# Shorter rests on GpSimd between indirect transfers in a routed mixture of experts

## The chip, the cores and the metric

The kernel runs on one core of a Trainium2 chip. The metric is the device time of one execution in microseconds (us). A profile of one further execution comes with the runs. The engines are called PE (TensorE), DVE (VectorE), ACT (ScalarE), POOL (GpSimd) and SP (SyncE, which here only issues DMAs); PEld is the weight load of PE.

## The reference, cut to what matters

Eight blocks are applied one after another to 2048 tokens of 128 numbers (8 sequences of 256), each as `x = layernorm(x + block(x))`: attention and feed-forward blocks L0 to L3. The change lies in the sixth, a mixture of 160 experts of which each token takes 8:

```python
def _L2_ffn_ref(hidden_states, router_w, expert_bias, w_gate, w_down, w_gate_shared, w_down_shared):
    ...
    probs = jax.nn.sigmoid(x @ router_w.T + expert_bias[None, :])
    top_w, top_idx = jax.lax.top_k(probs, 8)
    top_w = top_w / (jnp.sum(top_w, axis=-1, keepdims=True) + 1e-09) * 2.5
    combine = zeros(T, 160) with top_w at top_idx
    h1 = jax.nn.silu(jnp.einsum('th,eih->eti', x, w_gate))
    routed = jnp.einsum('eti,ehi->th', h1 * combine.T[:, :, None], w_down)
    return routed + silu(x @ w_gate_shared.T) @ w_down_shared.T
```

The block after it (L3 attention) is six layers of linear attention and a feed-forward of 512; the last (L3 ffn) is attention with weights of several widths.

## The kernel before, in words

The tokens are four groups of 512 (`GT`), held as tiles of 128 partitions x 4 x 128. Two groups make a half: `first` is groups 0 and 1, `second` groups 2 and 3. The halves go through the blocks staggered, so that one half's work can run beside the other's.

In the routed experts the work of a half has four steps:

- `plan` counts the tokens of each expert and gives every (token, choice) pair a row in a table in DRAM, `placed[h]`. Rows are grouped in tiles of 64 of one expert, eight tiles to a block. `place` then scatters the tokens: for each group 4 x 8 indirect DMAs on GpSimd (L622), each of 128 rows of 512 bytes, so 64 per half.
- `routed_experts` runs 36 blocks: 20 with one tile for each of the 160 experts, 16 with the tiles that overflow, whose experts are known only at run time. A block loads its rows (`xb`, L702) and weights (L713, L714, or eight loads at L719), turns the rows (L725), multiplies (L729, L740) and writes the results to a second table, `made[h]` (L743, issued by ACT). A block that is not used skips its transfers. Weights and rows have two buffers each. The load of the first block waits for all the scatters of its half.
- `gather` fetches for each token its eight rows from `made[h]` (L751), again 64 indirect DMAs per half, into `got` (two buffers of eight), and DVE adds them up, weighted (L757). It waits for the last write of `made[h]`.
- The normalized sum goes to the six layers of L3 attention (matmuls at L1106 to L1171; the feed-forward of a layer is L1165 and L1171).

`pause` (L541 is its `memset`) stands behind every indirect DMA: fills of a scratch tile `idle` (128 x 176) on GpSimd, tied in order to the transfer before and the transfer behind, so that GpSimd rests between two transfers. Nothing reads `idle`.

The order of the program around it, from the end of the kernel's body:

```python
            stage(run, l2_route, first)
            plan(first)
            l1_experts(second)
        routed_experts(first)
        ...
        stage(run, l2_route, second)
        plan(second)
        gathers(first)
        es.close()
        layers = l3_attn(ctx)
        run = layers(first)
        routed_experts(second)
        ...
        gathers(second)
```

`plan(h)` holds the scatters of the half. `l3_attn(ctx)` issues the loads of the L3 weights on SP's queue (L63, L69). Each engine runs its instructions in an order fixed when the program is built by a scheduler with a cost model; `behind` adds an order without a wait.

Of the kernel before, what the change touches and what calls it, by code (L numbers as in the profile page):

```python
# [42 lines left out]
def tile_post_ln_blocks(ctx: ExitStack, tc: tile.TileContext, I, out: bass.AP):  # L43
    nc = tc.nc
    V, S, G, PE = nc.vector, nc.scalar, nc.gpsimd, nc.tensor
# [98 lines left out]
    def tokens(g, src):  # L144
        t = xs[g].tile([P, 4, D], F32, tag="x", name="x")
        normalize(g, t, src)
        return t
# [384 lines left out]
    def behind(ins, other, why):  # L532

        tc.add_manual_dep(
            ins, other.name, mybir.DependencyInfo(mybir.DependencyClass.NoSync, mybir.DependencyReason.DATA), reason=why
        )

    def pause(after):

        for _ in range(3):  # L540
            after, last = G.memset(idle, 0.0).ins, after  # L541
            behind(after, last, "a rest between transfers")
        rest[0] = after

# [20 lines left out]
    def plan(half):  # L565

        n = EXPERTS

        def t(tag, dt=F32):
            return pp.tile([P, n], dt, tag=tag, name=tag)  # L570

        c0, c1 = (count[g] for g in half)
        whole, size, end, jump = t("whole", U32), t("size"), t("end"), t("jump")
        V.tensor_tensor(size, c0, c1, ALU.add)
        V.tensor_scalar(size, size, TILE - 1.0, TILE - 1.0, ALU.add, ALU.max)
        V.tensor_copy(whole, size)
        V.tensor_scalar(whole, whole, 0xFFFFFFFF - (TILE - 1), None, ALU.bitwise_and)

        V.tensor_scalar(size, whole, -float(TILE), 0.0, ALU.add, ALU.max)
        V.tensor_tensor_scan(end, ones, size, 0.0, ALU.mult, ALU.add)  # L580
        et = pp.tile([P, 1], F32, tag="et", name="et")
        own = t("own_c")
        V.scalar_tensor_tensor(own, end, tile_at, ones, ALU.is_le, ALU.mult, accum_out=et)
        pe = bank(lanes[0].ps)[:1, :P]
        PE.transpose(pe, et, ident)
        ei = pp.tile([1, P], I32, tag="ei", name="ei", bufs=2)
        V.tensor_copy(ei, pe)

        V.tensor_tensor(end, end, size, ALU.subtract)
        V.scalar_tensor_tensor(jump, end, TILE * (n - 1.0), first_at, ALU.add, ALU.subtract)  # L590
        placing[half[0] // 2] = []
        tile_of[half[0] // 2] = ei
        for g, c in zip(half, (None, c0)):
            place(lanes[g % 2], g, c, jump)

    def place(ln, g, before, jump):
        n, k, h = EXPERTS, TOP, g // 2
        at = upto[g]
        if before is not None:
            V.tensor_tensor(at, at, before.unsqueeze(1).to_broadcast([P, 4, n]), ALU.add)  # L600
        far = parts(ln, "gw", n)[0]
        V.scalar_tensor_tensor(
            far, at, float(TILE), jump.unsqueeze(1).to_broadcast([P, 4, n]), ALU.is_gt, ALU.mult
        )
        V.tensor_tensor(at, at, first_at.unsqueeze(1).to_broadcast([P, 4, n]), ALU.add)
        V.tensor_tensor(at, at, far, ALU.add)
        V.tensor_tensor(at, at, chosen[g], ALU.mult)
        p8 = ln.pick.tile([P, 4, 8], F32, tag="p8", name="p8")
        for j in range(4):
            V.max(out=p8[:, j, :], in_=at[:, j, :])  # L610

        p, q, rw = (ln.pick.tile([P, 4, k], U32, tag=f"pl{i}", name=f"pl{i}") for i in range(3))
        V.tensor_scalar(p, p8[:, :, :k], -1.0, None, ALU.add)
        V.tensor_scalar(rw, p, P - 1, 2, ALU.bitwise_and, ALU.logical_shift_left)
        V.tensor_scalar(q, p, 7, 3, ALU.logical_shift_right, ALU.bitwise_and)
        V.tensor_tensor(rw, rw, q, ALU.bitwise_or)
        V.tensor_scalar(p, p, 0xFFFFFFFF - (TILE * BLOCK - 1), None, ALU.bitwise_and)
        V.tensor_tensor(rw, rw, p, ALU.bitwise_or)
        row[g] = rw
        for j in range(4):  # L620
            for c in range(k):
                i = G.indirect_dma_start(  # L622
                    placed[h][:, :], bass.IndirectOffsetOnAxis(rw[:, j, c : c + 1], 0), x[g][:, j, :], None
                ).ins
                group = f"place{h}"
                if placing[h]:
                    tc.declare_no_dep(i, group=group, reason="no two tokens have the same row")
                tc.add_to_no_dep_group(group, i)
                placing[h].append(i)
                if rest[0] is not None:  # L630
                    behind(i, rest[0], "a rest between transfers")
                pause(i)
        placed_at[g] = at, p8

    def shares(ln, g):
# [109 lines left out]
    def gather(ln, g):  # L745

        y = sums[g]
        for j in range(4):
            got = gp.tile([P, 8, D], F32, tag="got", name="got")
            for c in range(TOP):  # L750
                i = G.indirect_dma_start(  # L751
                    got[:, c, :], None, made[g // 2][:, :], bass.IndirectOffsetOnAxis(row[g][:, j, c : c + 1], 0)
                ).ins
                behind(i, rest[0], "a rest between transfers")
                pause(i)
            for c in range(TOP):
                V.scalar_tensor_tensor(  # L757
                    y[:, j, :], got[:, c, :], share[g][:, j, c : c + 1], y[:, j, :], ALU.mult, ALU.add
                )
        x[g] = tokens(g, y)  # L760
# [22 lines left out]
    def parts(ln, tag, *sizes):  # L783

        t = ln.work.tile([P, sum(4 * n for n in sizes)], F32, tag=tag, name=tag)
        at, out = 0, []
        for n in sizes:
            out.append(t[:, at : at + 4 * n].rearrange("p (a b) -> p a b", b=n))
            at += 4 * n
        return out  # L790
# [580 lines left out]
    def gathers(half):  # L1371
        for g in half:
            gather(lanes[g % 2], g)

    with ExitStack() as moe:
# [9 lines left out]
        idle = mw.tile([P, 176], F32, tag="idle", name="idle")  # L1385
# [64 lines left out]
    last = l3_ffn(ctx)  # L1450
# [140 lines left out]
```

## Time and profile before

| | us |
|---|---|
| median of 3 runs | 2006.09 |
| lowest, highest | 2005.3, 2006.96 |
| profiled execution, device time | 2013.03 |
| its span in the trace | 2011.1 |

| engine | busy us | share of the span |
|---|---|---|
| PE | 1742.4 | 87% |
| PEld | 1166.6 | 58% |
| DVE | 1211.9 | 60% |
| ACT | 889.9 | 44% |
| POOL | 453.2 | 23% |

The profiled execution takes 1.9 us more than its span. Times in the trace are from the start of the span. Of POOL's time, 191.6 us are the 768 fills of L541 (249 ns each), 127.5 us the 128 scatters of L622 and 123.2 us the 128 gathers of L751. The profile's duration of an indirect DMA is the time that POOL is occupied by it; its data land later.

### The profile page before, as it was taken

How to read it: one execution, taken by the hardware profiler on the slowest of the kernel's cores; microseconds unless marked ns; L12 is line 12 of the kernel's file. 1: busy time of each engine (PE TensorE's matmuls, PEld its weight loads, DVE VectorE, ACT ScalarE, POOL GpSimd, SP SyncE). 2: the span in 40 equal slices, each digit the busy share in tenths (PEclk: the TensorE clock that was granted, in tenths of full speed). 3: DMA queues.
4: the chain of work that ended last, by engine and by line, in shares of the span. 5: the costliest groups of instructions: out<-in, count | busy, mean ns of one | idle time of the engine just before them, and what ended most of it. 6: DMA issues, size and time to landing. Idle time of an engine off the chain costs nothing.

```text
span 2011.1 us, 38559 instructions
## 1 busy us (share of the span) xinstructions
PE 1742.4 (87%) x13996; PEld 1166.6 (58%) x13996; DVE 1211.9 (60%) x3920; ACT 889.9 (44%) x1992; POOL 453.2 (23%) x1041
## 2 busy tenths in 40 slices
PE   9999889977999999999879672677967799999887
PEld 6888644554555446644467451556745677666554
DVE  4000356876878756799558720455576777766663
ACT  4555434724755345642424210133444466555543
POOL 1000000000000000007870688883088400000000
PEclk9999989988999999999789866778988899999997
DMA  3000078502333642336118765777011000000000
GB/s 100 4 3 4 22 227 255 168 0 59 105 100 99 164 128 76 100 106 188 46 44 262 239 192 175 236 223 219 31 33 32 19 1 1 1 1 6 6 1 11
DMA packets 161486, 185.38 MB, mean 92 GB/s; under 512 B 20336, under 2 KB 118512, under 8 KB 161296
## 3 DMA queue, kind: packets, MB, share of 16 engines
q1 hardware_dynamic: 143264, 149.86, 25.9%
q0 software_dynamic: 8192, 16.79, 2.7%
q10 hardware_dynamic: 9840, 16.26, 2.2%
q8 instruction: 111, 1.82, 0.4%
q14 instruction: 79, 0.65, 0.1%
HBM read 143.69 MB, written 56.16 MB: 99 GB/s over the span
## 4 chain that ended last, share of the span: by engine, by line
PE 60%; POOL 17%; DVE 10%; DMA 5%; issue 4%; ACT 4%; SPq 0%; ACTq 0%; POOLq 0%; DVEq 0%
PE ps_s L360 8%; POOL idle L541 7%; PE ps_o L427 7%; PE ps_m L432 7%; POOL placed L622 6%; PE ps_m L437 4%; PE ps L136 4%; PE ps L1171 4%; POOL got L751 3%; PE ps L1165 3%; PE ps_s L279 2%; DMA got<-made,pl 2%; PE ps L956 2%; PE ps L1294 2%; PE ps_o L740 1%
## 5 line engine op out<-in xcount | busy, mean ns | idle before, releaser
L622 POOL DMA_INDIRECT placed<-x,pl x128 | 127.5, 996 | 998.5 <-DMA wu<-in_F_wu_dram 903.6
L434 ACT ACTIVATE h<-ps_m 128x512 f32<-128x512 f32 x196 | 116.0, 597 | 235.7 <-PE ps_m L432 213.6
L427 PE MATMUL ps_o<-h,wd 128*128 128x512 f32 x384 | 200.9, 607 | 7.8 <-DVE h L440 7.8
L432 PE MATMUL ps_m<-xT,wg 128*128 128x512 f32 x384 | 197.9, 598 | 3.0 <-ACT h L434 3.0
L541 POOL MEMSET idle<- 128x176 f32 x768 | 191.6, 249 | 29.7
L360 PE MATMUL ps_s<-st,L_a 128*64 128x32 f32 x4096 | 193.2, 222 | 1.1
L360 PEld LDWEIGHTS ps_s<-st,L_a 128*64 128x64 f32 x4096 | 160.7, 137 | 29.9 <-ACT st L369 12.3
L440 DVE TENSOR_TENSOR h<-h,bc 128x512 f32<-128x512 f32 x192 | 131.4, 686 | 48.8 <-ACT h L434 40.3
L369 ACT ACTIVATE st<-ps_s 128x64 f32<-128x64 f32 x512 | 114.2, 223 | 102.6 <-PE ps_s L360 71.1
L751 POOL DMA_INDIRECT got<-made,pl x128 | 123.2, 963 | 104.3 <-DMA made<-ob 78.3
L437 PE MATMUL ps_m<-xT,wu 128*128 128x512 f32 x256 | 133.8, 605 | 4.2 <-ACT h L434 2.8
L740 PE MATMUL ps_o<-w,xg 64*64 64x128 f32 x1152 | 102.1, 331 | 37.6 <-DVE xg L735 37.4
L427 PEld LDWEIGHTS ps_o<-h,wd 128*128 128x128 f32 x384 | 73.2, 195 | 96.9 <-issue 66.6
L432 PEld LDWEIGHTS ps_m<-xT,wg 128*128 128x128 f32 x384 | 71.2, 191 | 84.7 <-issue 64.7
L438 DVE TENSOR_TENSOR h<-h,ps_m 128x512 f32<-128x512 f32 x132 | 89.9, 681 | 46.8 <-PE ps_m L437 43.3
L740 PEld LDWEIGHTS ps_o<-w,xg 64*64 64x64 f32 x1152 | 80.4, 165 | 57.0 <-DVE xg L735 46.8
L317 DVE SCALAR_TENSOR_TENSOR outsT<-xnT,L_skip,ps 128x64 f32<-128x64 f32 x32 | 10.4, 324 | 168.2 <-PE ps L305 168.2
L742 ACT COPY ob<-ps_o 128x512 f32<-128x512 f32 x72 | 42.1, 585 | 154.8 <-PE ps_o L740 139.5
L136 PE MATMUL ps_m<-ident,xb 128*128 128x128 f32 x288 | 57.5, 333 | 58.9 <-DMA xb<-placed 58.9
L757 DVE SCALAR_TENSOR_TENSOR yb<-got,w,yb 128x128 f32<-128x128 f32 x128 | 44.3, 346 | 103.4 <-DMA got<-made,pl 102.9
L1165 PE MATMUL ps<-nT,A_w 128*128 128x512 f32 x192 | 98.1, 632 | 9.5 <-ACT nT L1091 5.2
L1171 PE MATMUL ps<-A_w,hT 128*128 128x128 f32 x768 | 99.1, 281 | 6.5 <-DVE hT L1167 6.4
(370 smaller groups left out, 3603.5 us busy)
## 6 DMA issues: line engine op xcount, KB each, us to landing
bc<-comb SPq DMA_DIRECT2D x128, 256.0 KB
w<-in_F_w_dram SPq DMA_DIRECT2D x256, 96.0 KB
placed<-zero SPq DMA_DIRECT2D x72, 256.0 KB
xb<-placed SPq DMA_DIRECT2D x72, 256.0 KB
made<-ob ACTq DMA_DIRECT2D x72, 256.0 KB
w<-in_F_wg_dram SPq DMA_DIRECT2D x40, 256.0 KB
w<-in_F_wd_dram SPq DMA_DIRECT2D x40, 256.0 KB
bc<-comb SPq DMA_DIRECT2D x16, 512.0 KB
```

What stands on the lines that cost most here:

```text
L136: PE.transpose(ps[:, j, :], src[:, j, :], ident)
L360: in_turn(PE.matmul(now[h][sides[c], n % HB // 2, n % 2, s].rearrange("p e f b -> p (e f b)"), lhsT=a_sb[:, n % 2, 4 * h + k, :], rhs=prev ...
L427: PE.matmul(acc[g], lhsT=w, rhs=h, start=begin, stop=end, skip_group_check=True)
L432: PE.matmul(pg, lhsT=wg, rhs=xT[g], start=True, stop=True)
L437: PE.matmul(pu, lhsT=wu, rhs=xT[g], start=True, stop=True)
L440: V.tensor_tensor(h, h, bc[:, i * GT : (i + 1) * GT], ALU.mult)
L541: after, last = G.memset(idle, 0.0).ins, after
L622: i = G.indirect_dma_start(placed[h][:, :], bass.IndirectOffsetOnAxis(rw[:, j, c : c + 1], 0), x[g][:, j, :], None).ins
L740: PE.matmul(po[k, i // 2, :], lhsT=h[k, i // 2, :], rhs=wd[i], start=True, stop=True)
L751: i = G.indirect_dma_start(got[:, c, :], None, made[g // 2][:, :], bass.IndirectOffsetOnAxis(row[g][:, j, c : c + 1], 0)).ins
L1165: PE.matmul(ph, lhsT=w1[:, f * P : (f + 1) * P], rhs=nT, start=True, stop=True)
L1171: PE.matmul(po[:, j, :], lhsT=hT[:, f, j * P : (j + 1) * P], rhs=w2[:, f, :], start=(f == 0), stop=(f == 3),)
```

## The change

The rest becomes a parameter. Behind the scatters of the first half it stays three fills of 176 columns; behind those of the second half and behind the gathers of both halves it becomes two fills of 112 columns.

```diff
-    def pause(after):
-
-        for _ in range(3):
-            after, last = G.memset(idle, 0.0).ins, after
+    def pause(after, fills=3, columns=176):
+
+        for _ in range(fills):
+            after, last = G.memset(idle[:, :columns], 0.0).ins, after
             behind(after, last, "a rest between transfers")
         rest[0] = after
...
-                pause(i)
+                pause(i, *((3, 176), (2, 112))[h])
...
-                pause(i)
+                pause(i, *((2, 112), (2, 112))[g // 2])
```

## The prediction

> **What bounds the kernel now.** I read the chain of waits first, to see whether POOL is on the path at all.
>
> ```profile
> PE 60%; POOL 17%; DVE 10%; DMA 5%; issue 4%; ACT 4%; SPq 0%; ACTq 0%; POOLq 0%; DVEq 0%
> ```
>
> POOL is busy for only 23% of the span, but 17% of the chain is POOL's: 7% the fills of `idle` (L541), 6% the scatters (L622), 3% the gathers (L751). The chain in order of time is POOL nearly throughout 911 to 1045 us (first scatter, left as it is), 1117 to 1248 (second scatter), and much of 1455 to 1586 (second gather). Then the timeline of POOL, for one transfer and its rest:
>
> ```profile
> 1119.70 0.96 POOL L622 DMA_INDIRECT placed<-x,pl  x1 [0.16 <-issue]
> 1120.66 0.86 POOL L541 MEMSET idle<- 128x176 f32 x3
> 1121.69 0.96 POOL L622 DMA_INDIRECT placed<-x,pl  x1 [0.16 <-issue]
> ...
> 1483.14 0.95 POOL L751 DMA_INDIRECT got<-made,pl  x1 [0.16 <-issue]
> 1484.09 0.86 POOL L541 MEMSET idle<- 128x176 f32 x3
> ```
>
> Columns: start, duration, what, idle before it. A transfer costs 0.96 + 0.86 (three fills) + 0.16 = 1.98 us. Every eighth gap is 0.48, so the 64 of the second scatter take 1117.71 to 1247.8, 2.03 each. Nothing but POOL's own stream paces them. Next, the busy time by stage, for what happens beside it (PE, PEld, DVE, ACT, POOL, then granted clock, DMA share, GB/s):
>
> ```profile
> 1180.00:1218.00 38.00, 30.77 (x332) 23.59 (x332) 9.74 (x18) 8.71 (x18) 31.00 (x73) 0.81 0.38 121
> 1218.00:1251.00 33.00, 0.51 (x10) 0.27 (x6) 0.00 (x0) 0.58 (x1) 27.55 (x65) 0.56 0.73 226
> 1455.00:1587.00 132.00, 92.62 (x442) 65.33 (x440) 91.52 (x339) 53.66 (x127) 110.24 (x256) 0.87 0.11 33
> 1587.00:2011.00 424.00, 386.35 (x2354) 265.61 (x2354) 283.71 (x918) 226.32 (x537) 0.00 (x0) 0.94 0.01 3
> ```
>
> From 1218 to 1251 everything but POOL stands still: the first half's experts are done, the second half's tokens are not placed. After 1587 PE is 91% busy. The timeline of SP's queue says what it does in the hole:
>
> ```profile
> 1216.19 0.34 SPq L63 DMA_DIRECT2D A_wk<-in_A_wk_dram  x1
> ...
> 1235.84 0.38 SPq L714 DMA_DIRECT2D w<-in_F_wd_dram  x1
> 1248.35 4.30 SPq L702 DMA_DIRECT2D xb<-placed  x3
> ```
>
> From 1216 to 1236 it issues the L3 weights and the first two expert blocks' weights, one per 0.47 us; then it waits for the scatter until 1248.35 (the waits of SP's queue put 11.9 us down to it). The last wait that matters:
>
> ```profile
> POOL got L751 <- DMA made<-ob: 78.3, 1, 78.3
> ```
>
> The second gather starts at 1455.08, when the second half's experts have written their last block. So the order is: second scatter, experts of the second half (1250 to 1455), second gather (1455 to 1586), then 425 us in which PE is nearly full.
>
> **The price of a fill.** No row has 112 columns. The groups by shape give 98 ns for 128x1, 194 for 128x128, 249 for 128x176, 327 for 128x256. From 176 down at the slope 128-to-176 (1.15 ns a column) 112 cost 175; at the slope 176-to-256 (0.98) 186; from 128 down toward 128x1 (0.76) 182. I take 182. In a triple the fills are 0.27, 0.25, 0.24 with gaps of 0.05. Two of 112: 0.27 + 0.05 + 0.25 less 2 x 0.067 = 0.44, against 0.86. Saved: 0.42 us per transfer (0.40 to 0.44 by the other slopes), 27 us in each of the three stages (64 transfers each).
>
> That assumes the gap of 0.16 stays and the transfer stays at 0.96, and the trace has no transfer with less rest. Bounds: at worst the whole 0.42 comes back as waiting on POOL (saving 0), or the transfers stretch to 1.61, the longest in the first scatter (a loss of 0.23 each). I take no change, since all gaps within the scatter but one (1.49) are 0.16 or 0.48 whatever else runs, and the transfers average 964, 956 and 970 ns in the three stages, though the DMA share is 0.66, 0.73 and 0.11 there.
>
> By the Trainium skill, "DMA: Bandwidth & Descriptors", Anatomy of one DMA, a transfer from this queue has a fixed cost of about 2.0 us, mostly completion; transfers spaced by that would gain nothing here, because 1.98 is already it. The trace disagrees for spacing: the transfer at 1276.24 takes 3.43 us to land, and the next is issued at 1278.20, before that. Latency overlaps here.
>
> **Second scatter.** The last of 64 transfers starts at 1245.97 now; 63 x 0.42 earlier is 1219.5, and it lands 2.38 later as now, at 1222. What is late next? SP: its loads are in its queue ahead of the first `xb`, until 1236.2. So `xb` is read at 1236.3, not 1248.35: 12 us gained of the 27, and 15 us stay as a hole covered by SP's queue. Should these loads be placed elsewhere in the queue, the 27 come whole.
>
> **First gather.** It starts behind the scatter's last fill (1248.63); ACT's last write of `made` for the first half is issued at 1223.1, so it can start at 1224, and with 2.0 - 0.42 = 1.58 each its first group is complete at 1275 (now 1312), the second at 1325 (now 1377). No gain of its own; it lets the L3 layers of the first half begin 37 and 52 us earlier.
>
> **Experts of the second half.** 205 us now. Own blocks take 4.87 us each (11 `xb` loads, 1255.28 to 1308.91) until the first half's L3 work joins, and 6.1 after (6 loads, 1308.91 to 1345.56). That work now joins 37 - 12 = 25 us sooner, some 5 blocks at 1.24 more: 6 us lost. On the other side VectorE waits 41 us in this stage (75.8 less the 34.6 of the hole) for gathered rows, with the blocks' copies behind it in its queue; at 1.58 for 2.0 a fifth of it could go, 8 us, and I count half. Net: 2 us lost, bounds 6 lost to 8 gained.
>
> **Second gather.** 131 us now, on the path by the wait above; 27 gained. The two `got` buffers don't bind: every eighth gap is 0.48, as in the scatter, which has no such buffers. Eight transfers will take 12.7 us, and eight adds of 0.35 us fit.
>
> **Behind it.** The 425 us of the tail stay if the first half's L3 layers have come as far when the second gather ends. They have 58 of 192 matmuls of L1165 done by 1590. They will start 37 to 52 us sooner and the gather ends 37 sooner, so I take the tail as unchanged.
>
> Sum: 12 - 2 + 27 = 37 us off the profiled execution (span 2011.1, device time 2013.0). The median of the runs is 2006.1, 0.3% less; 2006 - 37 = 1969.
>
> **The rivals.**
>
> *The queue opens* (0.13): the loads of L3 weights don't stand before the second half's `xb`. For it: one of them (`A_wqv`) already sits at 1144 among the first half's blocks, so the order is not fixed by the code's. Against it: the rest go in one run of 20 us. 27 - 2 + 27 = 52 off: 1954.
>
> *The tail takes it back* (0.20): PE's work is conserved, and only its idle time can go. That is 12 us of the hole plus PE's idle share of the second gather, 30% of 27, 8 us: 20 off, 1986. For it: PE is 91% busy after 1587. Against it: the first half's layers get a longer stretch beside the experts, where PE was 71% busy (91.86 of 129 us).
>
> *Spaced by something else* (0.04): a drain of queued descriptors, or sequencer work hidden under the fills, keeps 1.98 us per transfer; then 2006. Against it: the overlap shown above, and DMA packets of this queue fill only 2.7% of the span, 54 us for 256 transfers, 0.21 each.
>
> *Transfers stretch* (0.09), the slower end: with less rest the descriptor work of each transfer is caught more by VectorE's traffic. The place is the second scatter and second gather, the price up to 1.61 a transfer. It decides from a mean of 0.96 + 0.42 = 1.38 on; at 1.61 each of the two stages on the path is 64 x 0.23 = 15 us longer, so 2036. For it: transfers of 1.3 to 1.6 come in 911 to 947, where VectorE is 98% busy (35.18 of 36 us). Against it: in the second gather VectorE is 69% busy and the mean is 970.
>
> [...]
>
> **How the numbers follow.** My forecast has 0.54, the rivals 0.13, 0.20, 0.04, 0.09. A difference under 0.2% (4 us) can't be told from none here. Faster is 0.54 + 0.13 + 0.20 = 0.87, same 0.04, slower 0.09. The range reaches past the first two rivals, from 1950 to 1990, and leaves the last two out; its own ends also hold the bounds of the fill (2 x 2 us) and of the experts' pace (-4, +10).
>
> **What would show it.** In the changed profile: fills 128x112 of about 182 ns, 384 of them, with 192 of 128x176 left; transfers still 0.96 with gaps of 0.16; the second scatter about 103 us, the second gather about 104. SP's wait for the placed rows gone, and `xb` read right behind the last weight load. The experts of the second half still about 205 us. The stretch from the second gather's end to the end of the span still about 425. Wrong would be: transfers over 1.38 us, gaps grown by the saved 0.42, L3 weight loads elsewhere in SP's queue, or a tail that is longer by more than 10 us.

## The result, and the profile after

The changed kernel takes 1989.98 us (median of four, 1988.37 to 1995.07); the kernel before took 2006.53 beside it. The ratio is 0.9922, with a 95% interval of 0.9903 to 0.9942: 16 us faster, where 37 were forecast. (Medians and ratios leave out three single runs of the experiments, of 2064 to 2074 us at a granted clock of 0.86, that fell into a slower state.) The profiled execution took 1988.37 us, with a span of 1986.6 (before: 2013.03 and 2011.1), so the two traces differ by 24.5 us; stages below are of the traces.

The chain of waits:

```profile
PE 19%; POOL 7%; DVE 6%; DMA 3%; issue 2%; ACT 2%; SPq 1%; ACTq 0%; DVEq 0%; POOLq 0%
```

Its shares add up to 40%: this chain was followed back only to about 1214 us, so it can't be set beside that of before as a whole. Within it POOL still has 7% (4.8% the gathers of L751 and 2.0% their fills, some 135 us).

The rest between transfers next. POOL's timeline (start, duration, what, idle before it) and its fills by shape, of the changed kernel:

```profile
1118.92 0.96 POOL L622 DMA_INDIRECT placed<-x,pl  x1 [0.16 <-issue]
1119.88 0.45 POOL L541 MEMSET idle<- 128x112 f32 x2
1120.50 0.96 POOL L622 DMA_INDIRECT placed<-x,pl  x1 [0.16 <-issue]
...
L541 POOL MEMSET idle<- 128x112 f32 x384 | 76.7, 200 | 11.1
```

The period is 1.58 us for 1.98; the transfer and its gap are what they were. Then SP's queue at the end of the second scatter, the busy time of the hole behind it (PE, PEld, DVE, ACT, POOL), and two waits:

```profile
1234.11 0.43 SPq L69 DMA_DIRECT2D A_bo<-in_A_bo_dram  x1
1234.85 0.33 SPq L702 DMA_DIRECT2D xb<-placed  x1
...
1218.00:1235.00 17.00, 1.04 (x16) 0.80 (x16) 1.41 (x4) 0.58 (x1) 12.60 (x30) 0.59 0.97 305
...
POOL got L751 <- DMA made<-ob: 111.1, 1, 111.1
DVE yb L757 <- DMA got<-made,pl: 74.4, 67, 10.0
```

The scatter ends at 1221.25 (1246.93 before), yet `xb` is read at 1234.85, behind the last weight load; from 1218 to 1235 PE is busy for 1 us. The hole is 17 us long, 33 before. The wait of POOL at L751 for the last block's `made` is still the one that starts the second gather. The wait of DVE for gathered rows, before:

```profile
DVE yb L757 <- DMA got<-made,pl: 102.9, 68, 34.6
```

It was 102.9 us in all, and is now 74.4. Then the stages: the second half's experts (first `xb` to second gather), the second gather, the stretch to the first half's output, the stretch to the end, and the last two together. Columns as in the prediction; before, then after:

```profile
1248.40:1455.10 206.70, 161.09 (x1528) 123.03 (x1529) 108.51 (x364) 65.88 (x138) 108.98 (x257) 0.80 0.58 179
1455.10:1585.30 130.20, 91.25 (x437) 64.26 (x436) 91.12 (x337) 52.97 (x125) 109.47 (x253) 0.88 0.11 32
1585.30:1810.60 225.30, 213.96 (x1254) 155.52 (x1255) 165.55 (x555) 132.74 (x324) 0.75 (x4) 0.96 0.01 1
1810.60:2011.10 200.50, 173.66 (x1110) 111.06 (x1106) 118.56 (x365) 94.27 (x216) 0.00 (x0) 0.92 0.02 6
1585.30:2011.10 425.80, 387.62 (x2360) 266.58 (x2359) 284.10 (x919) 227.01 (x539) 0.75 (x4) 0.94 0.01 4
```

```profile
1234.90:1437.70 202.80, 159.47 (x1600) 122.63 (x1601) 118.17 (x408) 73.55 (x156) 77.30 (x172) 0.88 0.61 188
1437.70:1541.70 104.00, 76.96 (x339) 53.55 (x337) 73.27 (x270) 41.63 (x98) 86.48 (x190) 0.82 0.14 41
1541.70:1755.20 213.50, 203.37 (x1179) 146.60 (x1180) 159.02 (x534) 128.87 (x313) 0.43 (x3) 0.97 0.01 1
1755.20:1986.60 231.40, 191.44 (x1207) 125.11 (x1205) 129.52 (x404) 102.58 (x237) 0.00 (x0) 0.90 0.02 5
1541.70:1986.60 444.90, 394.81 (x2384) 271.71 (x2384) 288.54 (x938) 231.44 (x549) 0.43 (x3) 0.93 0.01 3
```

`xb` comes 13.5 us sooner, the experts take 3.9 less, the gather 26.2 less, and the tail behind it is 19.1 longer. Up to the end of the second gather the changed kernel is 43.6 us ahead; it then gives back 19. The tail's two parts say where: the first half's output comes 12 us sooner behind the gather than before, but from there to the end it takes 31 us more, with 97 more matmul records in it and PE idle for 40 us instead of 27. The two halves run beside each other for less of the tail, and the second half is left with more to do alone.

That is an order of instructions, not a speed. The scheduler that fixes each engine's queue at build time costs the fills as well, so shorter fills gave another program: with the same instructions on PE, ACT, DVE and SP, their order differs from the end of the second scatter on. In PE's queue 459 of the second half's 612 matmul instructions of L3 attention stood ahead of the first half's very last matmul, which is one of its L3 ffn; now 427. In DVE's queue the adds of the first gather moved forward among the blocks' copies: the first eight of the 64 stood behind three of the second half's 36 blocks (L725), the last behind 26; now behind one and 20.

### The profile page after: what moved, and what is told of

It is laid out like the page before. It is cut to its first block, busy times and chain, and to the rows that moved or that the text cites. A ratio compares the mean times of both kernels' runs of the same rounds, so it can differ in the third digit from the quotient of the medians.

```text
span 1986.6 us, 38380 instructions
## 1 busy us (share of the span) xinstructions
PE 1738.6 (88%) x13996; PEld 1163.9 (59%) x13996; DVE 1209.9 (61%) x3920; ACT 890.6 (45%) x1992; POOL 385.1 (19%) x849
## 5 line engine op out<-in xcount | busy, mean ns | idle before, releaser
L434 ACT ACTIVATE h<-ps_m 128x512 f32<-128x512 f32 x196 | 116.0, 597 | 235.4 <-PE ps_m L432 213.7
L751 POOL DMA_INDIRECT got<-made,pl x128 | 122.7, 958 | 139.5 <-DMA made<-ob 111.1
L541 POOL MEMSET idle<- 128x112 f32 (+1 forms) x576 | 124.5, 216 | 18.5
L1165 PE MATMUL ps<-nT,A_w 128*128 128x512 f32 x192 | 100.0, 639 | 12.1 <-ACT nT L1091 6.2
L1171 PEld LDWEIGHTS ps<-A_w,hT 128*128 128x128 f32 x768 | 94.8, 198 | 15.3 <-DVE hT L1167 10.6
L729 PE MATMUL ps_m<-xg,w 128*64 128x64 f32 x1152 | 80.9, 259 | 16.3 <-DVE xg L725 7.9
```

What stands on the lines that cost most here:

```text
L434: gate = S.activation(h, pg, func).ins
L541: after, last = G.memset(idle[:, :columns], 0.0).ins, after
L751: i = G.indirect_dma_start(got[:, c, :], None, made[g // 2][:, :], bass.IndirectOffsetOnAxis(row[g][:, j, c : c + 1], 0)).ins
L1165: PE.matmul(ph, lhsT=w1[:, f * P : (f + 1) * P], rhs=nT, start=True, stop=True)
L1171: PE.matmul(po[:, j, :], lhsT=hT[:, f, j * P : (j + 1) * P], rhs=w2[:, f, :], start=(f == 0), stop=(f == 3),)
```

## The experiments

Theory: the order took back what the rests gave. Rival (the prediction's "tail takes it back"): PE's work is conserved and only PE's idle time could go, so about 20 us is all there is. To tell them apart, the order of one kernel was laid on the other's instructions: each engine's instructions were tied one behind the other, without waits, in the other program's order. All ratios are to the kernel before on the same chip.

**New rests in the old order, and old rests in the new.**

```diff
         tile_post_ln_blocks(tc, args, out)
+        pin_order(nc, tc)    # PE, ACT, DVE, SP: each instruction behind its predecessor in the other program
```

> The changed rests, with the order of the instructions on PE, ACT, DVE and SP pinned to that of the kernel before. Theory O (the 20 us that the tail gave back come from another order that the scheduler made of the shorter rests): the second gather ends 37 to 44 us sooner and the tail is 425 again, so the device time is about 1965, 20 to 25 below the changed kernel's 1990. Theory W (the tail gives back whatever the second gather gains, because PE's work waits behind it in any order): about 1988, as the changed kernel.

> The rests of before, with the order of the changed kernel pinned. Theory O: the second gather ends near 1586 and the tail is 445 as in the changed kernel, so about 2025, slower than before by 1%. Theory W: the order is harmless, about 2006.

Measured: 1974.92 us, ratio 0.9835 (0.9804 to 0.9866) with the new rests, and 2060.46, ratio 1.0266 (1.0231 to 1.0301) with the old. The same change is worth 33 us where the order is kept: 10 us short of the 1965 that the theory said, and far below the 1988 of its rival. In the first, the experts took 187.6 us, though `xb` was read only at 1245.17 (the old order puts four weight loads of blocks ahead of it), and the tail was 430.2. In the second, an order made for gathers with short rests met gathers with long ones: the experts took 235.4 us, DVE waited 150.0 us for gathered rows, and the tail was 439.7 (425.8 with the same rests in the old order). The theory had the direction and nearly the tail; its 2025 counted the tail alone and missed the experts.

**One stage at a time, old order.** The edit is one pair of the two tables in the diff of the change:

```diff
-                pause(i, *((3, 176), (2, 112))[h])
+                pause(i, *((3, 176), (3, 176))[h])         # scatter: old rests
-                pause(i, *((2, 112), (2, 112))[g // 2])
+                pause(i, *((3, 176), (2, 112))[g // 2])    # gathers: the second alone
```

and so on for each stage.

> Short rests in the second scatter alone, order of before. The prediction's step (12 us gained, the rest of the 27 covered by SP's queue), if the parts add up: 1994. Theory W: the tail takes all but the PE idle time in the hole, also 12 off at most. If SP's queue did not cover: 27 off, 1979.

> Short rests in the second gather alone, order of before. Theory O and the prediction's step: 27 us off, 1979, the tail after the gather 425 as before. Theory W: only PE's idle share of the 27 us goes, 8 off, 1998, the tail 19 us longer.

> Only the first gather has short rests; all four engines keep the old order. The prediction gave this edit no gain of its own: 2006 to 2009, the second half's experts 207 us. The theory of the coupling (DVE's adds of gathered rows stand in its queue ahead of the experts' copies, so the gather's pace is the experts'): first gather 102 us for 127, experts of the second half 187 to 197 us for 206.7, second gather unchanged at 130, the time 10 to 20 us off, 1988 to 1999, a ratio of 0.990 to 0.995.

| short rests in | median us | ratio | second half's experts | second gather | tail |
|---|---|---|---|---|---|
| none (before) | 2006.5 | | 206.7 | 130.2 | 425.8 |
| second scatter | 1988.63 | 0.9902 (0.9865 to 0.9940) | 192.2 | 130.8 | 417.2 |
| first gather | 1991.23 | 0.9912 (0.9895 to 0.9928) | 189.8 | 129.9 | 421.4 |
| second gather | 1994.66 | 0.9929 (0.9905 to 0.9952) | 207.5 | 104.1 | 429.1 |
| all three | 1974.92 | 0.9835 (0.9804 to 0.9866) | 187.6 | 104.9 | 430.2 |

The first gather, to which the prediction gave nothing, shortens the experts by 17 us, as its coupling theory said. The short scatter did it by 14 without moving `xb` (1248.57, behind SP's weight loads): the first gather starts behind the scatter on POOL, at 1234.8, so rows are there sooner. Both act on one thing, the lead of the gather over the blocks, and don't add up in the experts: 192.2 and 189.8 us alone, 187.6 together. By the ratios the three single gains are 20, 18 and 14 us of 2006.5, the three together 33.

The second gather alone is 26 us shorter, but brings only 14, between the 27 and the 8 that were expected. The stretch behind it, with the scatter's rests short and the gather's long, then with the gather's short:

```profile
1571.60:1988.80 417.20, 379.13 (x2358) 261.73 (x2356) 284.28 (x919) 226.95 (x539) 0.75 (x4) 0.96 0.01 4
...
1561.60:1990.70 429.10, 387.75 (x2404) 268.00 (x2402) 292.35 (x948) 233.11 (x554) 0.53 (x3) 0.97 0.01 4
```

A short gather leaves PE less time beside it (77.2 us busy for 93.4), and what PE doesn't do there lies behind it: 46 more matmul records and 12 us more of tail, in one and the same order. The tail of before, 425.8, is no good measure for this, as its trace lost some 3 to 7 us to a lower clock in its last stretch (see the end of the next section); behind a long second gather the runs in the old order have 417.2 and 421.4.

**Which engine's order.** The same tie, laid on some engines only; the scheduler orders the rest anew.

```diff
-ORDER = {"PE": ..., "Activation": ..., "DVE": ..., "SP": ...}
+ORDER = {"PE": ...}
```

> The short rests of the change, with the old order of instructions kept on PE alone; ACT, DVE and SP are ordered anew. Theory (the order of PE's queue decides the length of the tail): the tail from the second gather's end to the end is 417 to 432 us as in the three kernels with the old order (430.2, 417.2, 429.0), and since SP reads the first xb ahead of the block's weights here, as in the changed kernel, at about 1235 and not 1245, the time is 1960 to 1978, a ratio of 0.975 to 0.985. Rival (it is the order of DVE or ACT that lengthens the tail): tail 440 to 447, time 1985 to 1992.

> As the run with the old order on PE alone, but from the second half's first L3 matmul on, PE's queue has the new order (427 and not 459 of the second half's 612 matmuls of the L3 attention stand ahead of the first half's last one). Theory (the tail is longer because the two halves are interleaved less): tail 440 to 447, first output of the first half 30 to 50 us sooner, the time 12 to 20 us over that run, 1975 to 1993. Rival (what lengthens the tail is the order ahead of it, in the scatter and the experts): tail and time within 5 us of that run.

> Short rests; PE, ACT and DVE keep the old order, SP is ordered anew (it reads the second half's first xb ahead of that block's weights, as in the changed kernel). With the old order on PE alone the tail was 452.9 us and the time 2008.8. Theory (what lengthened it there is the order of ACT and DVE, which place the first half's L3 work against the experts): experts of the second half 187 to 197 us, tail 425 to 437, xb at 1235; the time 1958 to 1976, a ratio of 0.974 to 0.984. Rival (SP's order does it): experts 203 us or more, or a tail of 440 or more, 1985 or more.

> Short rests, the old order on DVE alone; PE, ACT and SP are ordered anew, and PE comes out with the two halves' L3 work interleaved as before (459 of the second half's matmuls ahead of the first half's last). With the old order on PE alone, and the same interleaving, the experts of the second half took 207 us and the tail 453. Theory (DVE's queue decides: its adds of gathered rows stand ahead of fewer or more blocks' copies): experts 178 to 192 us, tail 428 to 438, the time 1955 to 1975, a ratio of 0.973 to 0.984. Rival (the order of ACT decides): experts 200 us or more, tail 440 or more, 1990 or more.

| old order kept on | median us | ratio | `xb` at | experts | tail | DVE's waits for gathered rows |
|---|---|---|---|---|---|---|
| PE, ACT, DVE and SP | 1974.92 | 0.9835 (0.9804 to 0.9866) | 1245.2 | 187.6 | 430.2 | 9.1 |
| none (the change) | 1989.98 | 0.9922 (0.9903 to 0.9942) | 1234.9 | 202.8 | 444.9 | 74.4 |
| PE | 2008.79 | 0.9985 (0.9966 to 1.0005) | 1236.2 | 207.0 | 452.9 | 75.9 |
| PE, up to the second half's L3 | 2025.93 | 1.0078 (1.0056 to 1.0100) | 1236.0 | 208.4 | 474.6 | 74.9 |
| DVE | 1965.54 | 0.9781 (0.9753 to 0.9810) | 1244.7 | 190.9 | 426.4 | 11.0 |
| PE, ACT and DVE | 1957.02 | 0.9744 (0.9709 to 0.9779) | 1238.3 | 178.7 | 432.7 | 11.3 |

My theory of PE's queue alone fell: with PE's old order the kernel was no faster than before, and its tail longer still (452.9 us, beyond the 440 to 447 of the rival too). In that run DVE's adds stood early again, the first eight behind one of the second half's blocks and the last behind 18. With DVE's order laid on, the gain is 44 us. That run alone doesn't single out DVE, since the scheduler left PE, ACT and SP nearly in the old order too. The rows "PE" and "PE, ACT and DVE" come closer: in their programs PE's and SP's orders are one and the same, 35 of ACT's 1912 instructions and 270 of DVE's 3676 stand elsewhere, and the ratios are 0.9985 and 0.9744. The first and the last row differ only in SP's queue, by the place of two loads (the first `xb` ahead of blocks' weights, or behind them); their intervals don't overlap either. For the rows "DVE" and "PE, ACT and DVE" the theories held, except that the tail of the one is a little short (426.4 us, said 428 to 438) and the experts of the other are faster (178.7, said 187 to 197). The waits of the last row's kernel, and its stage of the experts, to compare with the waits and the first line of stages of the changed kernel:

```profile
DVE yb L757 <- DMA got<-made,pl: 11.3, 1, 11.3
...
1238.30:1417.00 178.70, 143.67 (x1526) 108.64 (x1527) 106.60 (x363) 65.61 (x138) 77.33 (x171) 0.90 0.66 213
```

DVE's timeline shows the mechanism. In the changed kernel:

```profile
1248.85 0.35 DVE L757 SCALAR_TENSOR_TENSOR yb<-got,w,yb 128x128 f32<-128x128 f32 x1 [0.65 <-DMA got<-made,pl]
1251.76 0.35 DVE L757 SCALAR_TENSOR_TENSOR yb<-got,w,yb 128x128 f32<-128x128 f32 x1 [2.56 <-DMA got<-made,pl]
1252.03 0.41 DVE L735 SCALAR_TENSOR_TENSOR xg<-xg,ps_m 128x256 f32<-128x256 f32 x1
1252.36 0.35 DVE L757 SCALAR_TENSOR_TENSOR yb<-got,w,yb 128x128 f32<-128x128 f32 x1
1252.62 0.68 DVE L725 COPY xg<-ps_m 128x512 f32<-128x512 f32 x1
```

and with the old order on PE, ACT and DVE:

```profile
1250.27 0.42 DVE L735 SCALAR_TENSOR_TENSOR xg<-xg,ps_m 128x256 f32<-128x256 f32 x1 [1.91 <-ACT xg L734]
1250.61 0.68 DVE L725 COPY xg<-ps_m 128x512 f32<-128x512 f32 x1
1251.21 0.73 DVE L757 SCALAR_TENSOR_TENSOR yb<-got,w,yb 128x128 f32<-128x128 f32 x2
1253.39 0.42 DVE L735 SCALAR_TENSOR_TENSOR xg<-xg,ps_m 128x256 f32<-128x256 f32 x1 [1.45 <-ACT xg L734]
```

In the first, a block's step at L735 has no idle time of its own: it is late because the add ahead of it waited 2.56 us for its rows. In the second, the adds find their rows and DVE waits only for the block itself. Between 1250 and 1350 us DVE made 20 of the blocks' copies in the changed kernel (20 before) and 24 here.

PE's order has a price too, in the tail. The rows "PE" and "PE, up to the second half's L3" differ in what is laid on PE from the second half's first L3 matmul on; the other engines are left to the scheduler in both, and DVE's and ACT's orders changed along with PE's, so the price is that of the three together. The stretch from the first half's output to the end, old order, then new:

```profile
1807.90:2000.40 192.50, 166.18 (x1110) 107.39 (x1106) 118.33 (x365) 94.38 (x216) 0.00 (x0) 0.97 0.02 6
```

```profile
1791.40:2023.20 231.80, 191.31 (x1206) 125.26 (x1204) 129.78 (x404) 102.65 (x236) 0.00 (x0) 0.91 0.02 5
```

The stretch ahead of it was 260.4 and 242.8 us: 17.6 us won there, 39.3 lost here, 22 in all (17 by the medians). The time grew by the 12 to 20 us that were expected, but the tail, 474.6 us, is far over the 440 to 447. The same long last stretch of 231 us is in the changed kernel and in the old rests with the new order, and in no kernel with the old interleaving (192 to 201). With DVE's order alone the scheduler came out with the old interleaving on PE again (459).

**No rest at all.** Old order, in the three stages of the change.

```diff
-                pause(i, *((2, 112), (2, 112))[g // 2])
+                pause(i, *((0, 112), (0, 112))[g // 2])    # the second scatter alike
```

> No fills at all in the second scatter and both gathers; old order on all four engines. If POOL's own stream alone paces the transfers: period 0.96 + 0.16 = 1.12 us and 0.04 for the longer gap at every eighth, second scatter and second gather about 75 us each (104 to 105 with the short rests), transfers still 0.96 us. The scatter's share stays behind SP's queue of weight loads (xb at about 1245), the second gather's 29 us come off: about 1945, a ratio of 0.965 to 0.972. If transfers stretch without a rest (the rival of the prediction): mean of a transfer over 1.38 us, stages over 90 us, 1960 or more. If something else spaces them (descriptors in the queue, the 2.4 us of landing): the gap grows from 0.16 and the period stays over 1.4.

Measured: 1963.83 us, ratio 0.9770 (0.9750 to 0.9791). POOL's timeline and waits:

```profile
1120.60 0.96 POOL L622 DMA_INDIRECT placed<-x,pl  x1 [0.30 <-issue]
1121.87 0.96 POOL L622 DMA_INDIRECT placed<-x,pl  x1 [0.30 <-issue]
...
POOL got L751 <- DVE yb L757: 44.5, 9, 12.4
```

Transfers do not stretch, so that rival is out. But the gap grows from 0.16 to 0.30 us: the fill had covered 0.14 us of issuing. The scatter took 80.6 us, not 75, and the second gather 98.8: now the two `got` buffers bind, and POOL waits for DVE's adds (15.4 of the 44.5 us fall in this gather, the others in the first). Beyond the change's rests there are 6 us in that gather, and the tail behind it is 435.9 us for 430.2. So the 1945 that were expected are missed by 19 us.

**SP's hole, and the first scatter.** 25 of the 36 loads of L3 weights moved to ACT's queue; then also two fills of 112 in the first scatter; then these with the loads back on SP.

```diff
-        w = [[load(wp, f"A3_{k}{i}") for k in ("wqv", "wk", "wo", "w1", "w2")] for i in range(DEPTH)]
+        w = [[load(wp, f"A3_{k}{i}", by=S if i else None) for k in ("wqv", "wk", "wo", "w1", "w2")] for i in range(DEPTH)]
...
-                pause(i, *((3, 176), (2, 112))[h])
+                pause(i, *((2, 112), (2, 112))[h])
```

> Short rests and the old order on all four engines, but 25 of the 36 loads of L3 weights are issued from ACT's queue, among the first half's last blocks, and no longer stand in SP's queue ahead of the second half's first xb. The prediction kept 15 of the scatter's 27 us as a hole that this queue covers. If so: xb read at 1221 to 1228 (1245 with the same order and the loads on SP), experts still 187 to 195 us, tail 425 to 435, the time 12 to 20 us under the 1967.9 us of span there: 1948 to 1960, a ratio of 0.968 to 0.977. Rival (the experts end by the first gather's pace, since DVE's adds stand ahead of the blocks' copies): the experts grow by what xb gains, the second gather starts at 1427 to 1433 as before it, 1965 to 1975.

> As the run with 25 weight loads on ACT, with two fills of 112 columns in the first scatter as well, so in all 256 rests. The chain of waits is POOL nearly throughout 911 to 1045 us in the kernel before, so 64 x 0.42 = 27 us should come off ahead of everything else: first scatter 103 us, the time 20 to 27 us under that run, 1925 to 1940, a ratio of 0.956 to 0.967. Rival (the first half's experts wait for other work then, the shared experts or weights): under 10 us off.

> Two fills of 112 columns in all four stages, the weight loads back on SP's queue; PE, ACT and DVE keep the old order, SP is ordered anew. Moving the loads to ACT's queue had made the first half's experts end 13 us later, and the first scatter's short rests had then brought 12 us. Theory: the second scatter begins 10 to 14 us sooner than in the run with the same order and the first scatter's long rests, and all behind it with it: span 1940 to 1946, a ratio of 0.967 to 0.973. Rival (with xb of the second half held by the weight loads, the 12 us are hidden): as that run, 1955.

Measured: 1967.28 us, ratio 0.9803 (0.9770 to 0.9837); 1956.11, ratio 0.9754 (0.9711 to 0.9798); 1961.95, ratio 0.9777 (0.9740 to 0.9813). All three missed what their theories said. SP's queue with the loads on ACT:

```profile
1227.92 2.23 SPq L719 DMA_DIRECT2D w<-in_F_w_dram  x8
...
1237.02 7.78 SPq L702 DMA_DIRECT2D xb<-placed  x3
```

The last block of the first half was issued at 1227.9 (1214.4 in the changed kernel, 1221.8 with the same order and the loads on SP), so `xb` still came at 1237: the hole moved into the first half's experts. Of the 27 us of the first scatter, 13 reached the second scatter's start, and 7 the `xb` of the last kernel. With the loads on ACT the short first scatter brought 11 us (1956.11 for 1967.28, on one chip); but neither edit brought a gain that these intervals show over the kernel with the old order on PE, ACT and DVE.

That kernel, 1957.02 us at a ratio of 0.9744, beats both the kernel before and the changed one (0.9922).

## Why the prediction was wrong

**The step that failed** is "I take the tail as unchanged", and the assumption under it, that the queues keep their order when a fill gets shorter. The tail measured 444.9 us for 425.8. It failed in two parts. The prediction made the tail hang on how far the first half's L3 has come when the second gather ends (58 of 192 matmuls of L1165 by 1590; the trace has 56), and took it that an earlier start makes up for a shorter gather. It doesn't: with the old order kept, the tail is 417.2 and 421.4 us behind a long second gather (2358 matmul records) and 429.1 and 430.2 behind a short one (2404 and 2400). That is some 10 us with the order kept. The new order adds 15 (444.9 with 2384 records, for 430.2 with the same rests in the old order). There it isn't how much is left, but how the two halves share it; laying the new interleaving on PE cost 17 us by the medians, where the other engines were left to the scheduler.

**The rival that named the number, and a part of the cause.** "The tail takes it back" gave 1986, because PE's work is conserved. Part of that shows: behind a short second gather more of PE's work is left, and in the old order only 14 of the gather's 26 us were kept. But it isn't a floor, since with DVE's old order the same work took 1965.54. That its 1986 lies near the measured 1989.98 is luck: it counted neither the first gather's gain (18 us alone) nor the price of the new order (33 less 16 us), which have opposite signs.

**First gather, "no gain of its own"**, was wrong: 18 us by itself, in the old order. The profile before had shown where to look. The chain of waits of the kernel before, 1248 to 1455 us alone:

```profile
by line: POOL got L751 16.7%; POOL idle L541 13.3%; PE ps_o L740 9.6%; DMA xb<-placed 9.2%; DMA got<-made,pl 7.6%; issue 7.1%; PE ps_m L136 5.0%; PE ps_m L729 4.9%; PE ps L1165 4.2%; PE ps L1171 3.9%; PE ps L136 2.8%; DVE xg L725 1.9%; PE p
```

and of the kernel with the old order on PE, ACT and DVE, 1238 to 1417:

```profile
by line: PE ps_o L740 16.3%; DMA xb<-placed 12.9%; DMA made<-ob 12.1%; PE ps_m L729 6.3%; PE ps_m L136 6.3%; PE ps L1165 4.9%; PE ps L136 4.0%; PE ps L1171 3.9%; issue 3.6%; ACT ob L742 3.4%; DMA A_w<-in_A_w_dram 2.4%; DVE xg L725 2.4%; DVE
```

The gather, its fills and its landing were 38% of that chain, and are gone from these entries of the second. (In the changed kernel, 1235 to 1438, they are still 36%.) I had read the chain in 1117 to 1248 and 1455 to 1586 and passed over the stage between.

**Experts of the second half**: forecast 2 us longer with bounds of -8 to 6, measured 3.9 shorter in the changed kernel, inside. But the parts were mis-sized: of VectorE's 41 us of waiting there I let 4 go. With the old order on PE, ACT and DVE nearly all of it goes and the stage loses 28 us (206.7 to 178.7; 19 with the old order on SP too), and the new order of the adds took most of this back. Two errors of opposite sign made the term look right.

**Right**: the transfer at 0.96 and the gap at 0.16, so neither stretching nor other spacing. The fill came to 200 ns for the estimated 182; the period of 1.58 us was met, since the pair with its gap took 0.45 us for the estimated 0.44. The second gather took 104.0 us, as said. SP's queue covered half of the scatter's gain: `xb` at 1234.85, forecast 1236.3; the rival "the queue opens" did not happen. The first gather ran from 1224.3 to 1326.2, forecast 1224 to 1325. The sum of the first four steps was 37; they brought 43.6.

By the Trainium skill, "DMA: Bandwidth & Descriptors", Anatomy of one DMA, the fixed cost of about 2.0 us is mostly completion latency; spaced by it, a period of 1.58 would not be possible. The runs show periods of 1.58 and, without a rest, 1.26 us: the latency does not space these transfers.

**What stays open.** The two traces differ by 24.5 us and the medians by 16.5. In the profiled execution before, the last 1110 matmul records took 173.66 us at a granted clock of 0.92; in the other kernels with the old interleaving the same 1110 took 166 to 171 at 0.94 to 0.97. That is 3 to 7 us of clock, which fits the difference but isn't shown to be all of it. How the new places on PE, DVE and ACT share the 15 us of tail that the new order costs the changed kernel was not tried on the changed order itself.

## What to carry to other kernels

Where a scheduler orders the queues at build time by a cost model, a change of one duration is two changes: the duration, and a new order on every engine. Compare the orders of the two programs first; to price the edit itself, keep the old order and change only the duration. And read the chain of waits stage by stage, between the stages that one has in mind too: an engine that serves a stream in order (here VectorE, with adds of gathered rows between the blocks' copies) forces the pace of the slower stream on the faster one. And when a stretch is cut in which another engine works, what that engine no longer does there lies behind it: of the 26 us off the second gather, 14 were kept.

## What the runs showed of the hardware

A fill behind an indirect transfer hides part of the issuing of the next: the gap was 0.16 us with fills and 0.30 without, so that taking away the last 0.45 us of fills brought 0.32. GpSimd's fill of 112 columns took 200 ns, no less than that of 128 (194). The occupation of GpSimd by one indirect transfer stayed at 0.95 to 0.99 us on average in the second scatter and both gathers of every run, at periods from 1.26 to 1.98 us.
